# Attention's products turned by block reads a round behind their store, and gate and up rounded in three passes

## The chip, the cores and the metric

The kernel runs on one core of a Trainium2 chip. The metric is the device time of one execution in microseconds; before the change its median is 473.88 us over three runs (473.8 to 474.22). Names of engines: PE is TensorE (PEld its weight loads), DVE VectorE, ACT ScalarE, POOL GpSimd, SP SyncE, which here only issues DMAs. SPq and ACTq are their DMA issues.

## The reference

x has 4 sequences of 512 rows of 512 numbers. All is float32.

```python
q  = (layernorm(x) @ W_q.T).reshape(B, S, 16, 32)
kv = (layernorm(x) @ W_kv.T).reshape(B, S, 16, 32)
qf, kvf = l2_normalized(fft(q)), l2_normalized(fft(kv))     # over each head's 32
qv = qf * cumsum(kvf, axis=1)                               # running sum over the rows
x  = x + ifft(qv).real.reshape(B, S, D) @ W_o.T
h  = layernorm(x)
# weights are rounded to float8_e4m3fn, 1536 columns for gate and up
f  = silu((h @ fp8(gate_w)) * gate_scale) * ((h @ fp8(up_w)) * up_scale)
x  = x + (f @ fp8(down_w)) * down_scale
```

## The kernel before

**Rounds.** The rows are cut into 16 chunks of 128 (4 per sequence). The Fourier transforms are folded into the weights at the start. Then come rounds, one per chunk, written out by hand as a software pipeline: nothing reorders them, and each engine runs its instructions in the order of the code. Round i does, on PE, the two products of chunk i with the folded weights (`spectrum`, pq, L304), the turning of the products qv of chunk i-2 (`v_transpose`, pt_v, L273: four 128x128 transposes), the row of chunk i+1's means (`x_row`, L292), the running sum of chunk i-1 (`running`, cum, L359) and the output product of chunk i-2 (`project`, po, L399).

The other engines work between these. ACT squares the products (L315), takes the layer norm's sums (`stats`, L257 to L260), copies and splits in two parts. DVE subtracts the mean from x transposed (`x_center`, L296), sums squares (L320), scales by the norms (L328: kn and qn), adds the carried row (L342), splits (kl, L350), multiplies (L377 to L379) and adds the residual (L407). POOL raises to the power -1/2 (rn, L325; dev, L261) and combines real and imaginary parts (L387, L388). The last row of a running sum is carried to the next chunk by a small DMA that ACT issues (`carry`, row<-end, L368).

**Weights.** float8 rounding is done by arithmetic on units of 128x1024: 12 units for gate and up, 6 for down. Per unit there is an absolute value on ACT (L202) and four passes on DVE, called parts: step (exponent bits, L208), floor (L219), add (L223) and sub (L227), with a pass for overflow on ACT (L212) in the rounds or on POOL (L214) later. `given` says how many parts each round gets; `next_parts` issues them in three places of a round. The rest is done in the first steps of the FFN.

**FFN.** After the rounds come 48 steps (4 sequences x 12 blocks of 128 columns): `inner` makes gate and up (gu, L467), the fused product f (L478 to L485), `down` the product with the rounded down weights (pd, L500). Meanwhile the next sequence's rows are loaded, normalized and transposed: `y_blocks` stores the rows to DRAM and reads them back with the 32x32 blocks exchanged, in four DMAs (L439), and `y_turn` transposes within the blocks on DVE (L450). The first sequence's rows are transposed on PE (pt_f, L273). Running, products and output products of the last two chunks are put between the first steps (`on_pe`, `behind`).

**Queues.** All large DMAs are issued by SP in the order of the code, so one that waits holds up those behind it. Memory is given out by pools with a number of buffers per tag: x has 6, the scratch of `stats` and of `carry` share one buffer (tag "end").

Of the kernel before, what the change touches and what calls it, by code (L numbers as in the profile page):

```python
# [15 lines left out]
P = 128  # L16
HD = 32
# [4 lines left out]

E4M3_MIN_NORMAL = 2.0**-6
E4M3_OVERFLOW = 464.0
ROUNDER = 1.5 * 2.0**20
DOWN = 2.0**-40
HUGE = 2.0**127
# [3 lines left out]
def tile_fft_attention_then_fp8_ffn(  # L31
# [53 lines left out]

    chunks = [(b, c) for b in range(B) for c in range(TC)]
# [13 lines left out]
    def load_x(i):  # L100
        b, c = chunks[i]
        t = work.tile([P, D], F32, tag="x", name=f"x_{b}_{c}", bufs=6)
        nc.sync.dma_start(t, x[b, c * P : (c + 1) * P, :])
        xt[i] = t
# [23 lines left out]
    nc.gpsimd.memset(over, -E4M3_OVERFLOW * DOWN * HUGE)  # L128

# [13 lines left out]
    xn_all = dram.tile([B, TC, P, D], F32, name="xn_all")  # L143

# [41 lines left out]
    def load_unit(u):  # L186

        _, src, n, k = units[u]
        if k == 0:
            t = big_tile("rawf")  # L190
            if src is down_w:
                rows = src[n * KC * P : (n + 1) * KC * P, :]
            else:
                rows = src[:, n * D : (n + 1) * D]
            nc.sync.dma_start(t, rows.rearrange("(k p) n -> p k n", p=P))
            staged[u] = staged[u + 1] = t

    def quant_abs(u):
        k = units[u][3]
        w = staged[u][:, k : k + QH, :]  # L200
        a = work.tile([P, QH, D], F32, tag="qa", name=f"qa_{u}")
        nc.scalar.activation(a, w, AF.Abs, scale=DOWN)  # L202
        quant[u] = (w, a)

    def quant_step(u, in_rounds):
        w, a = quant[u]
        m = work.tile([P, QH, D], F32, tag="qm", name=f"qm_{u}")
        nc.vector.tensor_scalar(  # L208
            m.bitcast(I32), a.bitcast(I32), 0x7F800000, None, ALU.bitwise_and
        )  # L210
        if in_rounds:
            nc.scalar.activation(a, a, AF.Identity, scale=HUGE, bias=over)  # L212
        else:
            nc.gpsimd.tensor_scalar(a, a, -E4M3_OVERFLOW * DOWN, HUGE, ALU.add, ALU.mult)  # L214
        quant[u] = (w, a, m)

    def quant_floor(u):
        _, a, m = quant[u]
        nc.vector.scalar_tensor_tensor(m, a, E4M3_MIN_NORMAL * DOWN, m, ALU.max, ALU.max)  # L219

    def quant_add(u):
        w, a, m = quant[u]
        nc.vector.scalar_tensor_tensor(a, m, ROUNDER / DOWN, w, ALU.mult, ALU.add)  # L223

    def quant_sub(u):
        _, a, m = quant[u]
        nc.vector.scalar_tensor_tensor(units[u][0], m, -ROUNDER / DOWN, a, ALU.mult, ALU.add)  # L227
# [4 lines left out]
    for u in range(len(units)):  # L232
        parts += [(quant_floor, u), (quant_add, u)]
        if u + 1 < len(units):
            parts.append((quant_step, u + 1))
        parts.append((quant_sub, u))

    def next_parts(n, in_rounds=False):

        for f, u in parts[:n]:  # L240
            if f is quant_step:
                f(u, in_rounds)
                if in_rounds and units[u][3] == 0 and u + QH < U1:
                    load_unit(u + QH)
            else:
                f(u)
            if f is quant_add and u + 1 < len(units):
                quant_abs(u + 1)
        del parts[:n]


    def stats(src, name):

        less = work.tile([P, 1], F32, tag="less", name=f"less_{name}", bufs=4)
        rstd = work.tile([P, 1], F32, tag="dev", name=f"dev_{name}", bufs=12)
        each = work.tile([P, D], F32, tag="end", name=f"each_{name}", bufs=1)
        nc.scalar.activation(each, src, AF.Identity, accum_out=less)  # L257
        nc.scalar.activation(less, less, AF.Copy, scale=-1.0 / D)
        nc.scalar.activation(each, src, AF.Square, bias=less, accum_out=rstd)
        nc.scalar.activation(rstd, rstd, AF.Identity, scale=1.0 / D, bias=eps)  # L260
        nc.gpsimd.tensor_tensor(rstd, rstd, nhalf[:, 0:1], ALU.pow)  # L261
        return less, rstd
# [12 lines left out]

    def heads(t):
        return t.rearrange("p (h f) -> p h f", f=HD)


    st_x, rows, xns, pqs, sss, rns, qns, kns, carries, cums, qvs, qvTs, pos = (  # L280
        {} for _ in range(13)
# [4 lines left out]

    def x_stats(i):
        st_x[i] = stats(xt[i], nm(i))

    def x_row(i):  # L290
        rows[i] = ps.tile([P, KC, P], F32, tag="tp", name=f"row_{nm(i)}")
        nc.tensor.transpose(rows[i][:, 0, :], st_x[i][0].to_broadcast([P, P]), ident)  # L292
# [69 lines left out]
    def carry(i):  # L362

        if chunks[i][1] + 1 < TC:
            end = work.tile([P, D], F32, tag="end", name=f"end_{nm(i)}", bufs=1)
            nc.scalar.copy(end[P - 32 :, :], cums[i][P - 32 :, :])  # L366
            row = work.tile([1, D], F32, tag="row", name=f"row_{nm(i)}", bufs=1)
            nc.scalar.dma_start(row, end[P - 1 :, :])  # L368
            carries[i + 1] = row

    def products(i):

        qn, cum = qns.pop(i), cums.pop(i)
        qv = work.tile([P, D], F32, tag="qv", name=f"qv_{nm(i)}")
        cross = work.tile([P, D], F32, tag="cross", name=f"cross_{nm(i)}", bufs=1)
        qh, ch, xh = heads(qn), heads(cum), heads(cross)
        nc.vector.tensor_tensor(qv, qn, cum, ALU.mult)  # L377
        nc.vector.tensor_tensor(xh[:, :, :HK], qh[:, :, :HK], ch[:, :, HK:], ALU.mult)
        nc.vector.tensor_tensor(xh[:, :, HK:], qh[:, :, HK:], ch[:, :, :HK], ALU.mult)  # L379
        qvs[i] = (qv, cross)  # L380
# [9 lines left out]
    def v_transpose(i):  # L390
        pt = transpose(qvs.pop(i)[0], f"v{nm(i)}")
        qvTs[i] = work.tile([P, KC, P], F32, tag="qvT", name=f"qvT_{nm(i)}", bufs=1)
        nc.scalar.copy(qvTs[i], pt)
# [19 lines left out]
    def load_y(b):  # L413
        ys[b] = big_tile(f"ys_{b}")
        nc.sync.dma_start(ys[b], y_all[b].rearrange("c p d -> p c d"))

    def y_stats(b, c):
        st_y[b, c] = stats(ys[b][:, c, :], f"f{b}_{c}")

# [13 lines left out]
    def y_blocks(b, c):  # L433

        nc.sync.dma_start(xn_all[b, c], xns.pop(("y", b, c)))
        src = xn_all[b, c].rearrange("(i t) (k j f) -> j t k i f", t=HD, j=P // HD, f=HD)
        z = work.tile([P, KC, P], F32, tag="x", name=f"z_{b}_{c}", bufs=6)
        for j in range(P // HD):
            nc.sync.dma_start(  # L439
                z[j * HD : (j + 1) * HD].rearrange("t k (i f) -> t k i f", f=HD), src[j]  # L440
            )
        xns["z", b, c] = z

    def y_turn(b, c):
# [5 lines left out]
        nc.vector.transpose(t.rearrange("p k n -> p (k n)"), z.rearrange("p k n -> p (k n)"))  # L450
# [9 lines left out]
    def inner(n, on_pe, between):  # L460
# [19 lines left out]
        nc.vector.scalar_tensor_tensor(f, pgu[1], gus[:, 1, m : m + 1], g, ALU.mult, ALU.mult)  # L480
        fh = work.tile([P, S], F32R, tag="kh", name=f"fh_{b}_{m}", bufs=3)
# [7 lines left out]
    def down(steps):  # L489
# [17 lines left out]
        if steps[-1] % MC == MC - 1:  # L507
            for c in range(TC):
                o = work.tile([P, D], F32, tag="x", name=f"o_{b}_{c}", bufs=6)
# [31 lines left out]
    load_unit(0)  # L541
    spectrum(0, 1)
# [20 lines left out]
    next_parts(1, True)  # L563
# [8 lines left out]
    squares(1, 1)  # L572
    norms(1, 1)
    x_row(2)
    x_center(2)
    q_scaled(0)
    products(0)
    combined(0)
    spectrum(1, 0)
    squares(1, 0)  # L580
# [3 lines left out]


    given = [4 if i in (2, 5, 7, 9, 11) else 3 for i in range(N - 3)] + [2, 2, 0]
    for i in range(2, N):
        spectrum(i, 1)
        if i == N - 6:
            load_y(0)  # L590
        at(load_xT, i + 2)
        if i > 2:
            k_scaled(i - 1)
            finish(i - 3)
        at(load_x, i + 2)
        if i > 2:
            k_low(i - 1)
        squared(i, 1)
        v_transpose(i - 2)
        if i == 2:  # L600
            x_stats(3)
        next_parts(given[i] // 3, True)
        if i > 2:
            q_scaled(i - 1)
        summed(i, 1)
        norms(i, 1)
        if i == 2:
            q_scaled(1)
        for c in pair(i - (N - 4)):
            y_stats(0, c)  # L610
        spectrum(i, 0)
        next_parts((given[i] + 1) // 3, True)
        at(x_row, i + 1)
        running(i - 1)
        squared(i, 0)
        carry(i - 1)
        at(x_center, i + 1)
        products(i - 1)
        combined(i - 1)
        if i == N - 1:  # L620
# [7 lines left out]
        at(x_stats, i + 2)  # L628
        project(i - 2)
# [6 lines left out]
    for _, u in parts:  # L636
        if u not in staged:
            load_unit(u)
            if 1 not in ys:
                load_y(1)  # L640
    finish(N - 3)
    k_scaled(N - 1)
    k_low(N - 1)
    q_scaled(N - 1)

    def on_pe(n, part):
        if part == 0 and n < 2:
            v_transpose(N - 2 + n)
            if n == 1:
                finish(N - 2)  # L650
        elif part == 1 and n == 0:
# [3 lines left out]
            project(N - 2, "tp")  # L655
# [5 lines left out]
    def behind(n):  # L661
        b, m = divmod(n, MC)
        if n == 1:
            project(N - 1, "tp")
            finish(N - 1)
# [10 lines left out]
        if b + 1 < B and 0 <= m - 3 < TC:  # L676
            y_stats(b + 1, m - 3)


    for n in range(STEPS + 1):  # L680
        if n < STEPS:
            inner(n, on_pe, between)
# [70 lines left out]
```

## Time and profile before

| | |
|---|---|
| median of 3 runs | 473.88 us |
| profiled execution | 473.83 us, its span 471.8 us |
| PE busy | 459.6 us, 97% of the span |
| DVE busy | 285.8 us, 61% |
| ACT busy | 214.8 us, 46% |
| POOL busy | 200.9 us, 43% |
| DMA | 40.72 MB, mean 86 GB/s |

The span runs from the first to the last instruction of the profiled execution; 2.0 us of its time lie around it. The attention rounds take the span from about 25 to 196 us, the FFN's steps the rest. In the profile's rows "L296" is a line of the kernel, "xT<-xT,row" what is written and read, and brackets name the idle time of an engine just before a row and what ended it. Busy times of PE overlap a little, because matmuls are pipelined and their ends are modelled; distances between starts do not.

### The profile page before, as it was taken

The numbers are of one execution on the slowest core, as the hardware profiler recorded it, in microseconds if no ns is written. First come the engines' busy times: TensorE is split into PE (matmuls) and PEld (weight loads), VectorE is DVE, ScalarE is ACT, GpSimd is POOL, SyncE is SP. The second block draws the span as 40 slices with busy tenths as digits, with TensorE's granted clock in tenths as the row PEclk, the third lists the DMA queues.
The fourth block names the chain that finished last, engine by engine and source line by source line (L and its number), as shares of the span: only waits on it lengthen the run. The fifth ranks groups of instructions, "written<-read, shape, count | busy, mean of one in ns | idle before, by whom it ended". The sixth has DMA issues, their size and how long they took to land.

```text
span 471.8 us, 5001 instructions
## 1 busy us (share of the span) xinstructions
PE 459.6 (97%) x1736; PEld 314.4 (67%) x1736; DVE 285.8 (61%) x399; ACT 214.8 (46%) x418; POOL 200.9 (43%) x134
## 2 busy tenths in 40 slices
PE   6999999999999999999999999999999999999995
PEld 6534444444444444567888888888888888888884
DVE  1548989998898878776899453343433343523225
ACT  3556475656565874422763323643225533222220
POOL 0247999997998796631143240012220022400002
PEclk9999999999999999999999999999999999999999
DMA  8911424142451210525042031340050430200002
GB/s 283 364 50 40 156 67 157 67 156 68 158 181 43 68 45 22 200 90 156 25 96 60 1 103 76 77 90 12 0 180 25 95 61 0 90 0 1 0 0 89
DMA packets 46152, 40.72 MB, mean 86 GB/s; under 512 B 27696, under 2 KB 28080, under 8 KB 46128
## 3 DMA queue, kind: packets, MB, share of 16 engines
q1 hardware_dynamic: 45744, 40.39, 27.6%
q8 instruction: 13, 0.21, 0.2%
q10 hardware_dynamic: 384, 0.03, 0.1%
q14 instruction: 11, 0.09, 0.1%
HBM read 28.85 MB, written 11.53 MB: 86 GB/s over the span
## 4 chain that ended last, share of the span: by engine, by line
PE 77%; DVE 8%; ACT 7%; DMA 3%; issue 3%; POOL 2%; SPq 0%; DVEq 0%; ACTq 0%
PE gu L467 36%; PE pd L500 18%; PE pq L304 12%; PE po L399 6%; DMA row<-end 2%; ACT sq L315 1%; POOL rn L325 1%; PE pkv L152 1%; PE pt_v L273 1%; ACT end L366 1%; PE pw L167 1%; ACT qa L212 1%; DVE kn L328 1%; PE cum L359 1%; DVE kn L342 1%
## 5 line engine op out<-in xcount | busy, mean ns | idle before, releaser
L325 POOL TENSOR_TENSOR rn<-ss,nhalf 128x16 f32<-128x16 f32 x32 | 107.2, 3351 | 23.2 <-DVE ss L320 23.2
L480 DVE SCALAR_TENSOR_TENSOR f<-gu,gus,g 128x512 f32<-128x512 f32 x48 | 36.0, 749 | 107.2 <-PE gu L467 105.7
L467 PE MATMUL gu<-yh,wg 128*128 128x512 f32 x192 | 76.0, 396 | 0.0
L467 PE MATMUL gu<-yh,wu 128*128 128x512 f32 x192 | 74.9, 390 | 0.0
L500 PE MATMUL pd<-wd,fl 128*128 128x512 f32 x192 | 74.8, 390 | 0.0
L500 PE MATMUL pd<-wd,fh 128*128 128x512 f32 x192 | 74.8, 389 | 0.0
L467 PE MATMUL gu<-yl,wg 128*128 128x512 f32 x192 | 74.7, 389 | 0.0
L467 PE MATMUL gu<-yl,wu 128*128 128x512 f32 x192 | 74.7, 389 | 0.0
L483 ACT CAST fh<-f 128x512 fp32r<-128x512 f32 x48 | 29.8, 621 | 87.8 <-DVE f L480 87.8
L304 PE MATMUL pq<-wkv,xT 128*128 128x512 f32 x128 | 57.8, 594 | 0.9 <-DVE xT L296 0.9
L399 PE MATMUL po<-wo,qvT 128*128 128x512 f32 x128 | 57.6, 593 | 0.0
L304 PE MATMUL pq<-wq,xT 128*128 128x512 f32 x128 | 57.6, 592 | 0.0
L478 ACT ACTIVATE g<-gu,gus 128x512 f32<-128x512 f32 x48 | 33.0, 687 | 51.8 <-PE gu L467 50.7
L485 DVE TENSOR_TENSOR fl<-f,fh 128x512 fp32r<-128x512 f32 x48 | 35.8, 745 | 27.0 <-ACT fh L483 26.8
L512 POOL TENSOR_TENSOR o<-o,ys 128x512 f32<-128x512 f32 x14 | 17.7, 1291 | 80.6 <-DVE o L510 80.6
L304 PEld LDWEIGHTS pq<-wkv,xT 128*128 128x128 f32 x128 | 24.1, 190 | 30.7 <-issue 27.0
L467 PEld LDWEIGHTS gu<-yh,wg 128*128 128x128 f32 x192 | 36.1, 188 | 8.1 <-issue 0.5
L467 PEld LDWEIGHTS gu<-yl,wg 128*128 128x128 f32 x192 | 36.1, 188 | 8.1 <-issue 0.5
L500 PEld LDWEIGHTS pd<-wd,fl 128*128 128x128 f32 x192 | 36.0, 188 | 7.7 <-DVE fl L485 0.2
L500 PEld LDWEIGHTS pd<-wd,fh 128*128 128x128 f32 x192 | 36.0, 188 | 7.5
L467 PEld LDWEIGHTS gu<-yh,wu 128*128 128x128 f32 x192 | 36.1, 188 | 7.4
L467 PEld LDWEIGHTS gu<-yl,wu 128*128 128x128 f32 x192 | 36.1, 188 | 7.4
(84 smaller groups left out, 598.4 us busy)
## 6 DMA issues: line engine op xcount, KB each, us to landing
x<-in_x SPq DMA_DIRECT2D x16, 256.0 KB, 2.8
xT<-in_xT SPq DMA_DIRECT2D x16, 256.0 KB, 2.7
y_all<-x SPq DMA_DIRECT2D x16, 256.0 KB, 2.0
ys<-y_all SPq DMA_DIRECT2D x4, 1024.0 KB, 6.0
out<-o SPq DMA_DIRECT2D x16, 256.0 KB, 2.0
rawf<-in_gate_w SPq DMA_DIRECT2D x3, 1024.0 KB, 6.5
rawf<-in_up_w SPq DMA_DIRECT2D x3, 1024.0 KB, 5.5
rawf<-in_down_w SPq DMA_DIRECT2D x3, 1024.0 KB, 6.0
```

Source lines behind the costliest of these rows:

```text
L152: nc.tensor.matmul(pw[i][:, j * P : (j + 1) * P], lhsT=r[:, j, i * P : (i + 1) * P], rhs=fwd, start=True, stop=True,)
L167: nc.tensor.matmul(pw, lhsT=inv, rhs=r[:, j, :], start=True, stop=True)
L304: nc.tensor.matmul(pq, lhsT=xTs[i][:, k, :], rhs=w[:, k, :], start=k == 0, stop=k == KC - 1)
L325: nc.gpsimd.tensor_tensor(rns[i, j], sss.pop((i, j)), nhalf, ALU.pow)
L399: nc.tensor.matmul(po, lhsT=qvT[:, k, :], rhs=wo[:, k, :], start=k == 0, stop=k == KC - 1)
L467: nc.tensor.matmul(p, lhsT=w[:, k, m * P : (m + 1) * P], rhs=v[:, k, :], start=k == 0 and v is yhs[b], stop=k == KC - 1 and v is yls[b],)
L478: nc.scalar.activation(g, pgu[0], AF.Silu, scale=gus[:, 0, m : m + 1])
L480: nc.vector.scalar_tensor_tensor(f, pgu[1], gus[:, 1, m : m + 1], g, ALU.mult, ALU.mult)
L483: nc.scalar.copy(fh, f)
L485: nc.vector.tensor_tensor(fl, f, fh.bitcast(F32), ALU.subtract)
L500: nc.tensor.matmul(pds[b][c], lhsT=v[:, c * P : (c + 1) * P], rhs=wd[:, m, :], start=m == 0 and v is fused[n][0], stop=m == MC - 1 and v i ...
L512: add.tensor_tensor(o, o, ys[b][:, c, :], ALU.add)
```

## The change

- `v_transpose` goes. The products qv are stored to DRAM (`v_out`, at the end of their combination), read back in the next round by four DMAs with the 32x32 blocks exchanged (`v_back`), and transposed within the blocks by DVE in the round after (`v_turn`). `project` follows in that same round, one round later than before; three output products instead of two fall into the FFN's first steps.
- The two half cross products become one operation that reads the running sum's halves in reversed order.
- Gate and up units are rounded in three DVE passes (step, add, sub): a Relu with a large scale on ACT sums overflow into a column, which the add and sub take as the lower bound. Down units keep four.
- `stats` is split in `mean` and `deviation`; x's mean is taken a round before its deviation. The scratch has a tag of its own, and the carried row goes into the first row of its own tile.
- In each round SP issues the loads of x transposed, the store of y, the load of x, then weights (in halves of 512 KB, collected in `wanted`) and the first sequence's y (by chunk, from round 7 on), then the block reads. x has 7 buffers.
- Round 2 is written out by hand ahead of the loop, without an output product. `given` has 3 parts in most rounds, 2 in rounds 6, 8 and 10.

The core of the diff:

```diff
+    def blocks(z, there):
+        src = there.rearrange("(i t) (k j f) -> j t k i f", t=HD, j=P // HD, f=HD)
+        for j in range(P // HD):
+            nc.sync.dma_start(
+                z[j * HD : (j + 1) * HD].rearrange("t k (i f) -> t k i f", f=HD), src[j]
+            )
+    def turned(t, z):
+        nc.vector.transpose(t.rearrange("p k n -> p (k n)"), z.rearrange("p k n -> p (k n)"))
...
-    def v_transpose(i):
-        pt = transpose(qvs.pop(i)[0], f"v{nm(i)}")
+    def v_out(i):
+        nc.sync.dma_start(qv_all[i], qvs.pop(i)[0])
+    def v_back(i):
+        zs[i] = work.tile([P, KC, P], F32, tag="z", name=f"zv_{nm(i)}")
+        blocks(zs[i], qv_all[i])
+    def v_turn(i):
         qvTs[i] = work.tile([P, KC, P], F32, tag="qvT", name=f"qvT_{nm(i)}", bufs=1)
-        nc.scalar.copy(qvTs[i], pt)
+        turned(qvTs[i], zs.pop(i))
...
-        nc.vector.tensor_tensor(xh[:, :, :HK], qh[:, :, :HK], ch[:, :, HK:], ALU.mult)
-        nc.vector.tensor_tensor(xh[:, :, HK:], qh[:, :, HK:], ch[:, :, :HK], ALU.mult)
+        nc.vector.tensor_tensor(xh, qh, ch[:, :, ::-1, :], ALU.mult)
...
     def quant_abs(u):
...
+        if src is down_w:
+            nc.scalar.activation(a, w, AF.Abs, scale=DOWN)
+        else:
+            c = work.tile([P, 1], F32, tag="qc", name=f"qc_{u}")
+            nc.scalar.activation(a, w, AF.Abs, scale=UP)
+            nc.scalar.activation(m, a, AF.Relu, scale=FAR, bias=far, accum_out=c)
+            nc.scalar.activation(c, c, AF.Identity, scale=HUGE, bias=least)
...
     def quant_add(u):
+        if c is not None:
+            nc.vector.scalar_tensor_tensor(a, m, c, w, ALU.max, ALU.add)
...
-            row = work.tile([1, D], F32, tag="row", name=f"row_{nm(i)}", bufs=1)
-            nc.scalar.dma_start(row, end[P - 1 :, :])
-            carries[i + 1] = row
+            nc.scalar.dma_start(end[:1, :], end[P - 1 :, :])
+            carries[i + 1] = end[:1, :]
...
-    given = [4 if i in (2, 5, 7, 9, 11) else 3 for i in range(N - 3)] + [2, 2, 0]
-    for i in range(2, N):
+    given = [2 if i in (6, 8, 10) else 3 for i in range(N - 3)] + [2, 2, 0]
+    for i in range(3, N):
         spectrum(i, 1)
...
+        at(finish, i - 4)
         at(load_x, i + 2)
+        while wanted:
+            load_unit(wanted.pop(0))
+        if 0 <= i - (N - 9) < TC:
+            load_y(0, [i - (N - 9)])
+        v_back(i - 2)
+        k_low(i - 1)
+        v_turn(i - 3)
+        at(x_row, i + 1)
         squared(i, 1)
-        v_transpose(i - 2)
+        at(x_deviation, i + 1)
         next_parts(given[i] // 3, True)
...
         products(i - 1)
         combined(i - 1)
+        v_out(i - 1)
...
-        project(i - 2)
+        project(i - 3)
```

## The prediction

> **What bounds the kernel.** The page comes first: busy shares, then the span in slices.
>
> ```profile
> PE 459.6 (97%) x1736; PEld 314.4 (67%) x1736; DVE 285.8 (61%) x399; ACT 214.8 (46%) x418; POOL 200.9 (43%) x134
> PE   6999999999999999999999999999999999999995
> DVE  1548989998898878776899453343433343523225
> PEclk9999999999999999999999999999999999999999
> ```
>
> PE is busy for 459.6 of 471.8 us at the full granted clock, in every slice but the first and last. So time goes only where PE gets less to do or waits less. DVE runs at eight to nine tenths in slices 2 to 17, the attention rounds, so it is the engine that could take over there.
>
> Second, the timeline of PE over one round of attention (start, length, line, operation).
>
> ```profile
> 125.19 3.60 PE L304 MATMUL pq<-wkv,xT 128*128 128x512 f32 x8
> 128.62 0.60 PE L273 MATMUL pt_v<-tab,qv 128*128 128x128 f32 x4
> 129.06 3.60 PE L304 MATMUL pq<-wq,xT 128*128 128x512 f32 x8
> ...
> 133.06 3.60 PE L399 MATMUL po<-wo,qvT 128*128 128x512 f32 x8
> 136.50 3.60 PE L304 MATMUL pq<-wkv,xT 128*128 128x512 f32 x8
> ```
>
> The round is 136.50 - 125.19 = 11.31 us without a gap, and the four transposes delay the next product by 129.06 - 128.62 = 0.44 us (their 0.60 overlaps it). Starts are what counts, also on DVE, where a 0.68 us operation lets the next start after 0.60.
>
> Third, the same timeline at those places where PE does wait (idle time and releaser in brackets).
>
> ```profile
> 29.45 0.32 PE L292 MATMUL row<-tab,less 128*128 128x128 f32 x1 [0.32 <-ACT less L258]
> 33.60 3.70 PE L304 MATMUL pq<-wkv,xT 128*128 128x512 f32 x8 [0.39 <-DVE xT L296]
> 41.59 0.32 PE L292 MATMUL row<-tab,less 128*128 128x128 f32 x1 [0.38 <-ACT less L258]
> 187.15 0.63 PE L273 MATMUL pt_v<-tab,qv 128*128 128x128 f32 x4 [0.58 <-DVE yl L431]
> 200.61 0.50 PE L359 MATMUL cum<-kh,tri_r 128*128 128x512 f32 x1 [0.49 <-ACT g L478]
> ```
>
> The brackets understate it, because modelled ends overlap. By starts: a product of 3.43 us that began at 25.54 leaves 0.48 before 29.45, and the one from 29.61 leaves 0.56 before 33.60. The rounds from 33.60, 56.96 and 170.42 take 12.05, 11.70 and 12.55 us (the last with two y transposes of 0.44), so 0.74, 0.39 and 0.36 over 11.31. Near 187.15 0.75 is lost, near 200.61 0.5. Together 3.8 us.
>
> **The change: PE.** All 64 transposes of qv go: 14 rounds x 0.44, and two in the FFN at 0.35 (197.68 to 198.03): **-6.9 us**. Nothing replaces them on PE; every product stays, the output products (project) coming one round later and three instead of two of them falling into the FFN's steps. A round would then take 11.31 - 0.44 = 10.87 us; every other engine must fit into that.
>
> **DVE.** A StreamTranspose per chunk comes in, 0.70 long by the FFN's row below, 0.62 by starts. The cross products become one operation of 128x512: 0.60 like qv instead of 2 x 0.33. The rounding of gate and up loses its floor pass (1.14 by starts) in 12 units, and the rounds from number 5 on are given 25 parts instead of 32.
>
> ```profile
> core 0: us, PE busy (x) PEld busy (x) DVE busy (x) ACT busy (x) POOL busy (x), PEclk, DMA share, GB/s
> 117.20:128.50 11.30, 11.30 (x32) 5.47 (x32) 9.66 (x14) 6.57 (x12) 10.30 (x6) 1.00 0.48 165
> ```
>
> Such windows over rounds 5 to 15 average 9.70 us of DVE. By starts a round of before sums to kn 0.66, row add 0.60, x+po 0.60, kl 0.60, qn 0.66, two sums 1.20, xT 0.60, qv 0.60, cross 0.66 = 6.18, plus 32/11 parts x 1.0 (0.60 for the step, 1.14 for the three others) = 2.9: 9.1. The other 0.6 is operations stretched beside POOL (the 1.22 us passes reach 1.60). After: 6.18 + 0.62 - 0.06 + 25/11 x 1.0 + 0.6 = 9.6 of 10.87; a round with three parts 10.3. It fits with 0.5 to spare. The new passes' second operand (a column, a reversed read) has no row: between no change and +0.4 each (1.22 to 1.60). I take no change, since the old passes of the same form and size stand at 1.22.
>
> At this point a rule speaks against the change: the Trainium skill, "VectorE: DVE Perf Modes", section "Rules for kernel authors", sends a 128x128 transpose to TensorE when a PSUM destination is acceptable. Followed, the sum would lose its 6.9 us and end near 472; the rows above, where PE is full and DVE has 1.6 us idle per round, decide against it here.
>
> **POOL.** Its work is unchanged, but it stands in a ring with DVE: qn needs rn, the sum ss follows qn, rn follows ss.
>
> ```profile
> 121.49 3.82 POOL L325 TENSOR_TENSOR rn<-ss,nhalf 128x16 f32<-128x16 f32 x1 [0.93 <-DVE ss L320]
> 125.28 1.41 POOL L387 TENSOR_TENSOR qv<-qv 128x240 f32<-128x240 f32 x1
> 126.76 1.56 POOL L388 TENSOR_TENSOR qv<-cross 128x240 f32<-128x240 f32 x1
> 128.29 2.90 POOL L325 TENSOR_TENSOR rn<-ss,nhalf 128x16 f32<-128x16 f32 x1
> ...
> 132.64 3.82 POOL L325 TENSOR_TENSOR rn<-ss,nhalf 128x16 f32<-128x16 f32 x1 [0.92 <-DVE ss L320]
> ```
>
> Round trip 132.64 - 121.49 = 11.15, of which 1.45 is qn, ss and hand-over. Taking POOL's part plus 1.45 in the ten rounds from 66 to 180 us gives 9.8, 10.6, 10.5, 10.9, 10.3, 11.15, 10.7, 10.5, 11.1, 10.9: mean 10.64. Below 10.87, but only just; the excess of the long rounds is 0.5 us in all. The variance (dev) moves in front of rn(k), where POOL idles 0.9 already.
>
> **ACT.** Off: a 0.58 us copy per chunk, and the wait for the carry's DMA (ACT's first mean operation waits 13.0 us for it in five places), because the scratch tile is no longer shared. On, per gate or up unit: a Relu at about 1.15 in place of the 1.15 overflow pass, its accumulator read 0.19 and a column operation 0.29. ACT averages 6.8 us per round; at worst, with one y chunk's statistics (2.3) too, about 9.8. It fits. Loads in halves of 512 KB, x ahead of the weights in the queue (ACT waits 4.9 us for x), two more constants and the smaller scratch move no bytes and nothing that PE waits for: nothing, covered by the round in which x now lies ready early; uncovered, at most those 4.9.
>
> **DMA and SP.** Per round one more store of 256 KB and four block reads, whose issues take 0.63 us each on SP.
>
> ```profile
> DMA to landing us min/median/max: 2.2/2.5/3.7
> L450 DVE STREAM_TRANSPOSE t<-z x12: 697/704/705, 247.5 to 394.0; 128x512 f32<-128x512 f32 x12
> q1 hardware_dynamic: 9024, 2.10, 21.0%
> ```
>
> The last line is the DMA view of 230 to 275 us, where nothing but four such stores and sixteen reads run: 21% of 45 us = 9.45, so 2.4 us of all 16 engines per chunk, added to shares of 0.06 to 0.51. They fit. Latency: POOL ends the products about 3.1 us into the next round (128.3 against 125.19); store landed at 5.3, four issues until 7.9, landed at 10.4 to 11.6. DVE transposes after kl of the round after, about 3.9 us in, that is at 14.8: 3.2 us of cover. SP waits for the store with nothing urgent behind it: xT, y and x are issued first. If the cover went, each microsecond over it would stand in all 12 rounds.
>
> The Trainium skill, "DMA: Bandwidth & Descriptors", first table, puts line rate at 512 B and above; these pieces have 128 B. Measured or by rule, they are slow, and hidden.
>
> **The start.** Round 2 no longer holds an output product, so 3.9 us of PE cover are gone there. Against that, chunk 2's mean comes 1.2 us earlier (ACT starts it at 27.2 instead of 28.44) and chunk 3's some 7 us earlier. Followed with the same durations: PE has row 2 at 28.97, so its products for chunk 2 end at 39.5. DVE: rn(q0) is there at 32.8, qn, qv, cross and the two combinations end at 35.9, the sum at 36.5, kn of chunk 1 at 37.2, its row add at 37.9, kh on ACT at 38.5, kl at 39.2, chunk 2's sum at 39.8, the centring of chunk 3 at 40.4. So PE begins the k product of chunk 3 at about 40.5, where before stands, less product and transposes, at 45.65 - 3.87 = 41.8; and that of chunk 4 at 51.9 against 56.96 - 3.43 - 0.88 = 52.65. DVE's centring of xT arrives some 0.2 us after PE wants it both times. Bounds: all 2.2 us of early waits gain, or 3.9 us of cover lost. I take +1.2, the 0.39 of the round from 56.96 included.
>
> **The hand-over to the FFN.** The wait for yl goes with the transposes that shared its banks, and the carry of the last chunk no longer lands behind 4 MB of loads (5.5 us in the chain of waits): 0 to 1.6 us, I take 1.6. The FFN itself keeps 5.44 us per step on PE; its DVE work falls by four floor passes.
>
> **Sum.** 6.9 + 1.2 + 1.6 = 9.7, less 1.0 for rounds where the ring runs over (0.5) and DVE's late centrings (0.5): 8.7. The profiled execution took 473.83 us (span 471.8 plus 2.0), 0.05 below the median of 473.88. **473.9 - 8.7 = 465.2 us**; own range 463.2 (all 3.8 of waits gone: 6.9 + 3.8) to 467.0 (the transposes alone).
>
> **Rivals.** *The POOL ring sets the round.* If every round runs like that from 121.49, 11.15, then 12 x 0.28 = 3.4 comes back: 468.6. For: two of ten rounds are there. Against: the mean of 10.64. *The start gives its cover back:* 1.2 gained becomes 3.9 lost, 5.1 worse: 470.3. For: PE's two waits for less. Against: the earlier means. *Slower: DVE becomes the bound.* If beside POOL every pass costs its slowest row (1.60 twice, 1.19 for the step), the row add its 1.19 and the transpose 0.5 more, a round is 6.74 + 1.1 + 4.4 = 12.2, so 12 x 1.3 = 16 us worse: 481. It turns the gain into a loss from 10.87 + 8.7/12 = 11.6 us. For: rows of 1.60 and 1.19. Against: they never come together; the fullest of the windows of before holds 11.04. *The block reads do not take the transposes off PE*: excluded, the changed order holds no pt_v.
>
> **Chances.** Main 0.64, ring 0.17, start 0.09, DVE 0.10. The range goes to 470.3, which leaves out the slower case and the ends. 0.2%, about 0.95 us, is what a measurement can tell: faster 0.88, same 0.02, slower 0.10.
>
> **What would show it.** Right: no pt_v; starts of pq a steady 10.87 apart; PE busy near 453. Ring: PE or its weight load idle before pq behind DVE's xT, rn 3.8 in a row. DVE: busy over 10.8 of a round. Late reads: DVE idle before the transpose behind a DMA. A round of 11.3 or more would prove the sum wrong.

## The result, and the profile after

The changed kernel takes 469.61 us (median; 469.18 to 470.05), against 473.9 for the kernel before on the same chip: a ratio of 0.9908, 95% interval [0.9891, 0.9925], 4.3 us faster. Its profiled execution, the slowest of its four, took 470.05 us, with a span of 468.3; before, 473.83 and 471.8.

The page of the changed kernel: busy shares, two rows of the span in slices, and the shares of the chain that ended last.

```profile
PE 454.3 (97%) x1672; PEld 307.9 (66%) x1672; DVE 281.2 (60%) x387; ACT 213.2 (46%) x429; POOL 189.5 (40%) x133
PE   6999999999999989999999999999999999999995
POOL 0248887899778677620043140112210022400002
PE 66%; POOL 14%; DVE 9%; issue 5%; ACT 4%; DMA 1%; SPq 0%; ACTq 0%; DVEq 0%; POOLq 0%
```

PE has 64 instructions and 5.3 us less to do (459.6 to 454.3), but the span is only 3.5 shorter. Slice 15 of PE (164 to 176 us) shows an 8, and 14% of the chain is now POOL (2% before): for a while something other than PE sets the time.

The timeline of PE of the changed kernel gives the place: the starts of the k product (pq<-wkv) around the slow rounds, and the one long wait among them.

```profile
129.10 3.70 PE L368 MATMUL pq<-wkv,xT 128*128 128x512 f32 x8
141.36 3.70 PE L368 MATMUL pq<-wkv,xT 128*128 128x512 f32 x8 [0.42 <-DVE xT L360]
152.70 3.70 PE L368 MATMUL pq<-wkv,xT 128*128 128x512 f32 x8 [0.19 <-DVE xT L360]
164.31 3.70 PE L368 MATMUL pq<-wkv,xT 128*128 128x512 f32 x8 [0.46 <-DVE xT L360]
172.61 0.50 PE L423 MATMUL cum<-kh,tri_r 128*128 128x512 f32 x1 [1.06 <-ACT kh L409]
...
178.37 1.88 PE L368 MATMUL pq<-wkv,xT 128*128 128x512 f32 x4
```

From 63.79 to 129.10 six rounds take 10.88 or 10.89 each (the last 10.90), the 11.31 of before less 0.43. The next four take 12.26, 11.34, 11.61 and 14.06; the last holds 0.87 of y transposes (pt_f). Against 10.88 that is 1.38 + 0.46 + 0.73 + 2.31 = 4.9 us. From the last k product to the end of the span it takes 289.9.

What holds these rounds is read on POOL. Its timeline, changed kernel, over the turn that ends in the first slow round:

```profile
120.08 0.55 POOL L301 TENSOR_TENSOR dev_f<-dev_f,nhalf 128x1 f32<-128x1 f32 x1 [2.48 <-ACT dev_f L300]
120.60 1.18 POOL L449 TENSOR_TENSOR qv<-qv 128x240 f32<-128x240 f32 x1
121.86 0.70 POOL L450 TENSOR_TENSOR qv<-cross 128x240 f32<-128x240 f32 x1
122.51 3.36 POOL L389 TENSOR_TENSOR rn<-ss,nhalf 128x16 f32<-128x16 f32 x1
...
127.33 3.88 POOL L389 TENSOR_TENSOR rn<-ss,nhalf 128x16 f32<-128x16 f32 x1 [0.93 <-DVE ss L384]
132.87 0.95 POOL L301 TENSOR_TENSOR dev_f<-dev_f,nhalf 128x1 f32<-128x1 f32 x1 [1.65 <-ACT dev_f L300]
```

dev_f is the variance of the first sequence's y, which these rounds take along for the FFN. It stands in front of the combination (L449, L450) and the next rn; POOL waits 2.48 and 1.65 us for ACT's part of it. This turn of POOL takes 132.87 - 120.08 = 12.79 us.

The kernel before has dev_f at the same place on POOL, two at a time in rounds 12 and 13, and POOL does not wait there (no bracket):

```profile
159.64 1.08 POOL L261 TENSOR_TENSOR dev_f<-dev_f,nhalf 128x1 f32<-128x1 f32 x2
```

What the change moves, beside what its list names, is ACT's part. Before, ACT took y's statistics in these two rounds ahead of the second squares; now it takes those of one chunk in each of rounds 9 to 12, behind x's mean. Why ACT is late, its timeline and that of SP's issues in the changed kernel show:

```profile
129.81 0.63 ACT L291 ACTIVATE each<-x 128x512 f32<-128x512 f32 x1 [3.15 <-DMA x<-in_x]
...
132.50 0.29 ACT L300 ACTIVATE dev_f<-dev_f,eps 128x1 f32<-128x1 f32 x1
```

```profile
122.58 0.33 SPq L453 DMA_DIRECT2D qv_all<-qv  x1
...
123.93 0.42 SPq L110 DMA_DIRECT2D x<-in_x  x1
...
135.30 0.33 SPq L453 DMA_DIRECT2D qv_all<-qv  x1
```

ACT takes y's statistics behind x's mean, and that mean waits for x to land. The x load is issued by SP behind the store of qv, and that store waits for POOL's combination, which ends at 122.56 (121.86 + 0.70). So there is a ring: combination, store, x load (issued 123.93, awaited until 129.81), x's mean, y's statistics (to 132.79), dev_f, combination, next store at 135.30, 12.72 us after the first. Its longest link is the x load, 5.9 us from its issue to ACT's start (the median landing of the x loads is 4.1). It is a ring because three queues, SP's, ACT's and POOL's, each hold one piece behind another that it does not need.

### The profile page after: what moved, and what is told of

It reads as the page before. It is cut to its first block, busy times and chain, and to the rows that moved or that the text cites. A ratio compares the mean times of both kernels' runs of the same rounds, so it can differ in the third digit from the quotient of the medians.

```text
span 468.3 us, 5038 instructions
## 1 busy us (share of the span) xinstructions
PE 454.3 (97%) x1672; PEld 307.9 (66%) x1672; DVE 281.2 (60%) x387; ACT 213.2 (46%) x429; POOL 189.5 (40%) x133
## 3 DMA queue, kind: packets, MB, share of 16 engines
q1 hardware_dynamic: 82176, 48.79, 36.9%
## 4 chain that ended last, share of the span: by engine, by line
PE 66%; POOL 14%; DVE 9%; issue 5%; ACT 4%; DMA 1%; SPq 0%; ACTq 0%; DVEq 0%; POOLq 0%
PE gu L539 37%; PE pd L573 19%; POOL rn L389 10%; PE po L467 4%; PE pq L368 3%; POOL qv L449 2%; POOL qv L450 1%; DVE ss L384 1%; PE pkv L164 1%; ACT sq L379 1%; DVE wu L256 1%; DVE qv L440 1%; PE pw L179 1%; DVE cross L441 1%; DVE kn L392 1%
## 5 line engine op out<-in xcount | busy, mean ns | idle before, releaser
L389 POOL TENSOR_TENSOR rn<-ss,nhalf 128x16 f32<-128x16 f32 x32 | 105.5, 3297 | 14.1 <-DVE ss L384 14.1
L301 POOL TENSOR_TENSOR dev_f<-dev_f,nhalf 128x1 f32<-128x1 f32 x16 | 10.1, 629 | 88.0 <-ACT dev_f L300 86.3
L368 PEld LDWEIGHTS pq<-wq,xT 128*128 128x128 f32 x128 | 23.2, 190 | 27.8 <-issue 26.9
```

The lines of the kernel that those rows point to most:

```text
L368: nc.tensor.matmul(pq, lhsT=xTs[i][:, k, :], rhs=w[:, k, :], start=k == 0, stop=k == KC - 1)
L389: nc.gpsimd.tensor_tensor(rns[i, j], sss.pop((i, j)), nhalf, ALU.pow)
```

## The experiments

The theory: the 4.9 us of rounds 11 to 14 come from this ring, above all from dev_f's place on POOL, and all else of the forecast holds. Rivals: buffers of dev (y's four hold four of six); the norms on POOL being too long for rounds of 10.9, which the prediction had as its first rival; block reads that slow the x load; DVE at its bound. Each ratio is to the kernel before, with its 95% interval.

**More buffers for dev.** ACT waits 4.17 us at 162.50 for a buffer of dev that DVE's qn still reads. The kernel before had 12 of these buffers, the changed one has 6; the run goes back to 12.

```diff
-        rstd = work.tile([P, 1], F32, tag="dev", name=f"dev_{name}", bufs=6)
+        rstd = work.tile([P, 1], F32, tag="dev", name=f"dev_{name}", bufs=12)
```

> The changed kernel with 12 buffers instead of 6 for the reciprocal deviations (tag dev), nothing else. Theory A (the y statistics' chain sets the late rounds): the four y deviations hold four of the six buffers, so that chunk 14's deviation waits on ACT for chunk 12's qn (4.17 us in the trace); that wait goes, rounds 13 and 14 (11.61 and 13.19 us without the y transposes) come back towards 10.9, and the time falls from 469.6 by 1 to 2.5 us. Theory B (POOL and DVE stretch each other in the ring qn, ss, rn): the buffer is a symptom, the time stays within 0.3 us.

Measured: 470.25 us, 0.9914 [0.9899, 0.9929], no change against the 0.9908 of the changed kernel. In ACT's timeline of this run the long wait has moved:

```profile
161.63 1.15 ACT L237 ACTIVATE qa<-qa,over 128x1024 f32<-128x1024 f32 x1 [4.26 <-DVE qm L233]
```

The next instruction waits 4.26 us in its place, for a rounding step that stands on DVE behind the same late qn. So this wait was a symptom. The unchanged time alone does not prove it, because two things meet in this run's trace. Its rounds 11 to 14 take 11.40, 11.21, 10.98 and 13.51 us, 2.7 over 10.88 instead of 4.9. But its FFN is 1.7 us longer, with plain steps of 5.48 us instead of 5.44, and no run tells why. How much of the 2.2 us the buffers gave is open; in rounds 11 and 12 of the changed kernel nothing waits for one. That the 4.9 us do not need more buffers is shown by the next run, which has 6.

**y's statistics behind the norms.** On ACT and DVE the order of instructions stays as it was; only on POOL dev_f moves, from in front of the combination to behind the round's second rn.

```diff
-        if 0 <= i - (N - 7) < TC:
-            y_stats(0, i - (N - 7))
         at(x_center, i + 1)
         products(i - 1)
         combined(i - 1)
...
         norms(i, 0)
+        if 0 <= i - (N - 7) < TC:
+            y_stats(0, i - (N - 7))
```

> The changed kernel with each y chunk's statistics issued after the norms of q instead of before the products, so that POOL does its power for y after combining qv and after rn instead of before them; ACT keeps its order. Theory A: POOL no longer stands still 1.5 to 2.5 us in each of rounds 9 to 12 waiting for ACT's y deviation with the combination behind it, so rounds 11 and 12 (12.26 and 11.34 us) fall to about 11: 1.2 to 2.5 us off, 467.1 to 468.4. Theory B: POOL's work is the same and only 0.55 us per round of it moves: at most 0.5 us off.

Measured: 464.88 us, 0.9807 [0.9793, 0.9822], 4.7 us below the changed kernel. Its timeline of POOL (two rows), its chain of waits and its timeline of PE (two rows):

```profile
117.61 0.70 POOL L449 TENSOR_TENSOR qv<-qv 128x240 f32<-128x240 f32 x1
...
122.40 0.56 POOL L301 TENSOR_TENSOR dev_f<-dev_f,nhalf 128x1 f32<-128x1 f32 x1
```

```profile
PE 92%; DVE 3%; ACT 3%; issue 1%; DMA 1%; ACTq 0%; SPq 0%; DVEq 0%
```

```profile
150.87 3.60 PE L368 MATMUL pq<-wkv,xT 128*128 128x512 f32 x8
161.75 3.60 PE L368 MATMUL pq<-wkv,xT 128*128 128x512 f32 x8
```

The combination starts at 117.61 instead of 120.60, dev_f finds its input ready, POOL is gone from the chain, and every round from 63.83 to 161.75 takes 10.88; the one after holds 0.87 of y transposes and takes 11.75. Four instructions of 0.55 us in another place are worth 4.7 us. ACT's waits for x fall from 16.2 us to 6.6 by themselves. Run a second time in another comparison, it gave 464.78, 0.9814 [0.9801, 0.9827], and rounds of 10.88 again:

> The run with y's statistics first once more, beside the run above on one chip, so that the two stand in one comparison. If the 464.9 us are a property of the kernel, 464.5 to 465.3 and every round of attention 10.88 from number 5 to 14; if they were luck of that session, a round of 11.3 or more shows up between 129 and 176 us.

**The x loads a round early.** This cuts the ring at its other end: x no longer stands behind the store that waits for the combination.

```diff
+    load_x(5)
...
-        at(load_x, i + 2)
         while wanted:
             load_unit(wanted.pop(0))
...
         v_back(i - 2)
+        at(load_x, i + 3)
```

> The changed kernel with each load of x issued behind the block reads of the round before, ahead of the store of the products, instead of behind that store, the load of x transposed and the store of y; same buffers and bytes. Theory A: the load no longer waits on SP for POOL's combination, ACT's 16.2 us of waits for x fall below 3, the y statistics come 2 to 3 us earlier and rounds 11 and 12 fall to about 11: 1.2 to 2.5 us off, 467.1 to 468.4. Theory B: nothing that the ring needs comes earlier, within 0.3 us. If the DMA engines are simply full (theory C), x still lands 4 us or more after its issue and the waits only move.

Measured: 468.26 us, 0.9875 [0.986, 0.989]. ACT's waits for x fall to 6.5 us, all of them ahead of 54 us, and rounds 11 to 13 to 10.88, 11.07 and 10.98, so the load is a link of the ring. Round 14 stays long: 13.81, with the 0.87 of transposes. In it dev_f waits for nothing and still takes 1.25 us ahead of the combination (152.98 to 154.20 on POOL); qn, the rounding step, ACT's overflow pass and the carry follow late. The place on POOL therefore costs something even when its input is early. How the rest divides between the two links was not taken apart further.

**TensorE's transposes back, in both orders.** Store, block reads and DVE's transposes go; everything else of the change stays.

```diff
-        nc.sync.dma_start(qv_all[i], qvs.pop(i)[0])
+        pass
...
-        blocks(zs[i], qv_all[i])
+        pass
     def v_turn(i):
+        pt = transpose(qvs.pop(i)[0], f"v{nm(i)}")
...
-        turned(qvTs[i], zs.pop(i))
+        nc.scalar.copy(qvTs[i], pt)
```

In the change's own order:

> The changed kernel with the block reads undone alone: the products are transposed by PE again, at the place of the DVE transpose, and copied by ACT; no store, no read, everything else as changed. By the sum of the prediction the transposes cost 6.9 us of PE, so with all else equal 476.5. Theory A: without the store SP is not held up, x lands early, and at 11.31 us per round the chain of the y statistics (11.3 to 12.7 us) is nearly covered, so about 4 of the 4.9 us lost in rounds 11 to 14 come back: 471.5 to 473. Theory B: the ring has 11.31 us too and the same comes back; the two do not differ here, the run prices the block reads alone.

With y's statistics behind the norms:

> The order of the run with y's statistics first (464.9 us, every round 10.88), but qv turned by TensorE and copied by ScalarE again, without store and block reads. If the sum's 6.9 us for the transposes is right and nothing else of the round changes, 464.9 + 6.9 = 471.8, rounds of 10.88 + 0.44 = 11.32. If the better order is worth the same here as with the block reads, that is 4.7 below the 472.8 of the run with TensorE's transposes and the change's own order, 468.1 is what comes out. If the order only mattered because the store and the x load stand in one queue, it is worth nothing here: 472.8, within 0.5.

Measured: 472.81 us, 0.9974 [0.9964, 0.9985], and 472.1 us, 0.9965 [0.9953, 0.9977]. From number 6 to number 13 the rounds take 11.30 to 11.32 in both, and the two intervals overlap: without a store in front of the x load, with x landing in 2.8 and 2.9 us, and with 0.43 us more of PE's time in each round, y's place costs nothing that is sure. Which of the three does it was not taken apart. Against the run with y behind the norms, the transposes off PE are worth 472.1 - 464.9 = 7.2 us (7.5 by the two ratios); in the change's order only 472.8 - 469.6 = 3.2. These are prices of the whole exchange, with the store, the reads and DVE's transposes against ACT's copies. The rest of the change, without the block reads, gains about 1.2 us (0.9974).

**Reads of whole rows.** As many reads and bytes as in the changed kernel, in pieces of 2 KB instead of 128 B.

```diff
-        blocks(zs[i], qv_all[i])
+        for j in range(P // HD):
+            r = slice(j * HD, (j + 1) * HD)
+            nc.sync.dma_start(zs[i][r].rearrange("t k n -> t (k n)"), qv_all[i][r, :])
```

> The changed kernel, its order too, with the reads of v_back taking whole rows of 2 KB instead of pieces of 128 B; as many reads, as many bytes, and the exchange of the blocks is left out, so the output products get other numbers. If the pieces of 128 B slow the x load beside them (landing median 4.1 us in the changed kernel, 2.8 in the kernel before), x lands about 1.3 us earlier, each turn of the loop of rounds 11 to 14 is that much shorter, most of the 4.9 us come back: 465 to 467. If the loop is made of the order alone and the landing hardly matters, 469 to 470.

Measured: 468.9 us, 0.9898 [0.9876, 0.992]. The interval covers the changed kernel's 0.9908, so the pieces' size does not explain the 4.9 us; the six executions lie between 467.24 and 470.78, and a gain of up to 1.5 us can't be excluded. The DMA issues of this run (KB each, median us to landing):

```profile
x<-in_x SPq DMA_DIRECT2D x16, 256.0 KB, 4.2
zv<-qv_all SPq DMA_DIRECT2D x64, 64.0 KB, 4.5
```

In the changed kernel the two stand at 4.1 and 4.1. x lands no sooner beside large pieces.

**Four passes of rounding in the good order.** Gate and up are rounded as before the change; to keep the same work ahead of the FFN, ten passes more are issued.

```diff
-        if src is down_w:
+        if True:
             nc.scalar.activation(a, w, AF.Abs, scale=DOWN)
...
-        if units[u][1] is down_w:
+        if True:
             parts.append((quant_floor, u))
...
+    next_parts(1, True)
...
-    given = [2 if i in (6, 8, 10) else 3 for i in range(N - 3)] + [2, 2, 0]
+    given = [4 if i in (3, 4, 5, 7, 9, 11) else 3 for i in range(N - 3)] + [2, 2, 0]
```

> The order with y's statistics first, with the rounding of all weights in four passes as before, and 45 passes ahead of the feed-forward part instead of 35 (a round is given 3 or 4; six rounds have 4). By the prediction's sum VectorE then holds 7.34 + 3 x 1.0 = 10.3 us in a round with three and 7.34 + 4.0 = 11.3 in a round with four, against 10.88 of TensorE: up to 6 x 0.45 = 2.7 us slower than 464.9, so 465 to 467.6. If VectorE is nowhere near its bound (the three-pass rounding is not needed for the rounds of 10.88), 464.9 within 0.5. If it is the bound already in the rounds of 10.88, each of the ten passes more costs its 1.0: 474.

Measured: 470.88 us, 0.9944 [0.9931, 0.9956]: 6.0 slower than with three passes, and above the 467.6 that was expected at most from DVE's sum. From the k product of chunk 1 to that of the last chunk it takes 2.9 us more (176.08 - 25.09 against 173.50 - 25.37), of which one round, 12.57 long, holds 1.7; the hand-over to the first gate product takes 1.7 more (12.92 against 11.25); the rest of the FFN 1.75 more. DVE is busy for 10.7 to 11.2 us in five of rounds 5 to 11, which lose 0.7 us together; those given four passes take 10.88 to 10.99. In the long round, which has three, the overflow pass on ACT stands between DVE and the carry. DVE's timeline in the long round:

```profile
141.86 0.69 DVE L440 TENSOR_TENSOR qv<-qn,cum 128x512 f32<-128x512 f32 x1 [1.80 <-ACT end L430]
```

ACT waits 1.65 us for DVE's step, its overflow pass runs ahead of the carry's copy (end), and DVE waits 1.80 for that copy. So the third edit of the change is worth about 4.3 of the 6.0 us in this arrangement. A full DVE is the smaller part of it (0.7 in rounds 5 to 11); most of the loss in the rounds is again a matter of order, and what holds the hand-over was not followed. The 1.75 of the FFN is something else: its plain steps take 5.48 instead of 5.44 us, with PE busy throughout and the same instructions in PE's order, as in the run with 12 buffers for dev, whose rounding has three passes. No run tells why.

**The waits of the start.** Two centrings of xT taken forward on DVE, with x early and y behind the norms.

```diff
     spectrum(2, 1)
     x_row(3)
+    x_center(3)
+    k_low(1)
...
-    x_center(3)
...
         spectrum(i, 0)
+        if i == 3:
+            x_center(i + 1)
         next_parts((given[i] + 1) // 3, True)
```

> Y's statistics first and the x loads a round early together, and two centrings of xT taken forward on VectorE: that of chunk 3 ahead of k_low of chunk 1, where VectorE idles 0.68 us for ScalarE, and that of chunk 4 ahead of the rounding pass. TensorE waits 0.56 us for the one and 0.5 (by starts) for the other. If these waits are due to VectorE's order alone, 464.9 - 1.0 = 463.9, with the k product of chunk 3 at 39.9 instead of 40.5 and that of chunk 4 at 51.9 instead of 52.85. If what is late moves on to the lower part of k or to the products of the round (TensorE waits 0.23 for kl there), 464.4 to 464.9. The x loads by themselves should add nothing, since every round is TensorE's already.

Then also one rounding pass less ahead of kn at the end of round 2:

```diff
-    next_parts(2, True)
+    next_parts(1, True)
...
-    given = [2 if i in (6, 8, 10) else 3 for i in range(N - 3)] + [2, 2, 0]
+    given = [2 if i in (6, 8, 10) else 4 if i == 3 else 3 for i in range(N - 3)] + [2, 2, 0]
```

> The run with y first, x early and the two centrings ahead, with one more edit: the rounding's last pass at the end of round 2 (1.73 us beside POOL, ahead of kn of chunk 2) moves to the end of round 3, which is then given 4 passes instead of 3. If the 0.64 us that TensorE waited for kh at 47.14 in that run comes from this pass, kn is ready 1.7 us earlier, the wait goes, the k product of chunk 4 begins at 51.3 instead of 52.0, and the time is 0.7 us less: 464.0. If the pass that is moved makes round 3 or 4 late instead (the carry, the products), the time stays within 0.3 of 464.7, or 465.5 if both rounds lose.

Measured: 464.71 us, 0.9808 [0.9796, 0.9821], and 465.87 us, 0.9831 [0.9815, 0.9846]. Counted from the k product of chunk 1, the one of chunk 3 comes 0.73 us earlier than with y behind the norms alone (39.36 - 24.94 against 40.52 - 25.37), that of chunk 5 only 0.38 (63.02 - 24.94 against 63.83 - 25.37): PE waits 0.64 for kh in between. With the pass moved, chunk 4 comes 1.5 earlier and chunk 5 0.34 later, since the wait for kh (0.41) and one for xT stand one round on. The first gain can't be told from the run without it, the second edit gains nothing. The fastest version is the order with y behind the norms, with or without the forward centrings: about 464.8 us.

## Why the prediction was right, and where it was off

The direction was right, and the time lies in the range that goes to 470.3. That is partly luck. The sum's own range ended at 467.0, and the changed kernel came out 4.4 above the 465.2 that it named; the wide range reached so far only because the prices of the ring and the start were taken in, and neither came about as described. By the prediction's own sign, "a round of 11.3 or more would prove the sum wrong", the sum was wrong: four rounds took 11.34 to 14.06. The run with y behind the norms, 464.9, meets the named time with two errors that cancel, a start that gave nothing and overruns that did not come. By terms, on the spans:

- **Transposes, -6.9:** right. 7.2 us between the runs with and without them in the good order; rounds of 10.88 against the forecast 10.87. The reads come in time: DVE never waits for one before a transpose of the products.
- **Hand-over, -1.6:** right. From the last chunk's k product to the end of the span there were 471.8 - 182.97 = 288.8 us, and there are 289.9, with an output product of 3.43 more, two transposes of 0.35 and one of 0.44 less: 288.8 - 0.7 - 0.4 + 3.4 - 289.9 = 1.2, the two waits near 187 and 200 us. The remaining 0.4 is the wait in the round from 170.42, which is gone in the good order (11.75 there is 10.88 + 0.87).
- **Start, -1.2:** mis-sized; it gave about nothing. The k product of chunk 3 starts at 40.48, as forecast (40.5), but that of chunk 4 at 52.82 instead of 51.9, and at chunk 5 63.79 stands against 68.66 - 3.43 - 3 x 0.44 = 63.9. The step that failed followed DVE only to the centring of chunk 3. After it come a rounding pass of 1.72 (L256, beside POOL's combination; the bound was 1.60), and kn, kl and the centring of chunk 4 late behind it, as DVE's and PE's timelines of the changed kernel show:

```profile
43.73 1.72 DVE L256 SCALAR_TENSOR_TENSOR wg<-qm,qc,qa 128x1024 fp32r<-128x1024 f32 x1
```

```profile
52.82 3.70 PE L368 MATMUL pq<-wkv,xT 128*128 128x512 f32 x8 [0.24 <-DVE xT L360]
```

The run with that pass moved shows the link: chunk 4's product comes 1.1 us sooner than with the pass in place.

- **Overruns, +1.0:** the term that failed, in another place than it was put. It was 4.9 in rounds 11 to 14, and nothing in the good order. The step that failed is two sentences. "SP waits for the store with nothing urgent behind it: xT, y and x are issued first" holds within a round; the next round's x load does stand behind that store. And "at worst, with one y chunk's statistics (2.3) too, about 9.8. It fits" counts ACT's time, not the order: y's statistics stand behind an x mean that waits, and their last step stands on POOL ahead of the combination. The prediction looked at x's dev, which moved to where POOL idles. It did not look at y's, whose place on POOL stayed ahead of the combination while its input on ACT moved behind the mean of a late x.

The sum with these sizes: 6.9 + 0 + 1.6 - 4.9 = 3.6, against 471.8 - 468.3 = 3.5 measured. One reading is off without bearing on the sum: DVE's row shows eight or nine tenths in slices 4 to 14, and six to nine from there to 22.

**The rivals.** *The POOL ring sets the round* forecast 468.6, near the result, but not for its reason: in the good order rn still takes 3.52 to 3.88 where it took 3.88 and the rounds are 10.88. What was right in it is that POOL had little to give: the forecast's mean of 10.64 plus the 0.55 of a dev_f in that ring is 11.2, above 10.88, by estimate. Round 14 of the run with early x loads fits that, but no run shows it by itself. *DVE becomes the bound:* not with three passes: the add (L248) takes 1.27 in the mean, 0.05 above the 1.22 taken, and windows of the changed kernel hold up to 10.77 us of DVE in rounds of 10.88 without PE waiting.

```profile
core 0: us, PE busy (x) PEld busy (x) DVE busy (x) ACT busy (x) POOL busy (x), PEclk, DMA share, GB/s
74.68:85.56 10.88, 10.88 (x29) 5.00 (x28) 10.77 (x16) 6.29 (x14) 9.05 (x6) 1.00 0.62 168
129.10:141.36 12.26, 11.67 (x28) 4.83 (x27) 9.94 (x15) 8.80 (x21) 9.60 (x7) 1.00 0.58 136
```

The same view shows that no engine was short of time in the longest of these rounds but one: DVE 9.94, ACT 8.80 and POOL 9.60 of 12.26. *The start gives its cover back:* it gave back its gain, not the 3.9.

**The rules weighed.** The section "Rules for kernel authors" of the Trainium skill's "VectorE: DVE Perf Modes", which sends such a transpose to TensorE, does not pay in this kernel: 7.2 us are gained by taking it off a TensorE that is busy for 97% of the span. The section "Specifications" of "DMA: Bandwidth & Descriptors" (Trainium skill), with its line rate from 512 B up, speaks against pieces of 128 B. The traces agree that they cost the DMA engines time: the packets of SP's queue take 36.9% of the engines' span in the changed kernel and 33.5% with 2 KB pieces, for the same 48.79 MB. But the time of the kernel moved by 0.7 us only, inside the interval.

## What to carry to other kernels

Busy sums per round say whether work fits; they do not say whether it stands in the right place. For each instruction that a change moves, write down what now stands behind it on its engine, and follow the loop of queues until it closes: a load behind a store, a statistic behind that load, and a store behind that statistic make a ring, whose turn and not any engine's busy time is the round. When a wait goes by more buffers and another of the same length takes its place, look one engine further up. And when the time stays the same, compare the stages too: a gain in one can hide behind a loss in another.

## What was not expected of the hardware

The same instruction took quite different times: L256 1.27 to 1.72 us on DVE, rn 2.90 to 4.09 on POOL, both in the changed kernel. That DVE and POOL hold each other up is one reading, but rn also took 2.90 with DVE busy throughout (at 56.57), and no run separates it. The x load's landing went from 2.8 us before to 4.1 with one store and four reads more per round, back to 2.8 without them, and the size of the reads' pieces made no clear difference to it. And the FFN's plain steps of 5.48 instead of 5.44 us in two of the kernels, with the same PE order, stay unexplained.
